# Attention and FP4 feed-forward on one core: side products spread over the slots of the attention loop

## The chip, the cores and the metric

The kernel runs on one core of one Trainium2 chip. The metric is the time of one execution on the device in microseconds (us), the median of several. Within the core, five engines run their own instruction streams in order and meet at semaphores: TensorE (PE in the profile; its weight loads are PEld), VectorE (DVE), ScalarE (ACT), GpSimd (POOL) and SyncE (SP), whose queue issues nearly all DMA transfers here.

## The reference, cut to what matters

The input is x of 4 batches x 2048 rows x 256 columns, in float32. Multi-head attention (16 heads of 16) with rotary tables on all rows but the first 679, a residual, a layer norm, then a gated feed-forward whose operands are first rounded to FP4 values in blocks of 16, a residual and a second layer norm:

```python
qkv = (x @ w_qkv + b_qkv)                  # 256 -> 3 * 256, then q and k are rotated
attn = softmax(q @ k.T / sqrt(16))         # per batch and head: 2048 x 2048
x = layernorm(x + (attn @ v) @ w_proj + b_proj)
def fp4_linear(x, w): return fp4_quant_dequant(x) @ fp4_quant_dequant(w).T
gate, y = fp4_linear(x, w_gate), fp4_linear(x, w_up)          # 256 -> 704
x = layernorm(x + fp4_linear(silu(gate) * y, w_down))         # 704 -> 256
```

The rounding divides each block of 16 by a sixth of its largest magnitude, snaps to the grid 0, 0.5, 1, 1.5, 2, 3, 4, 6 and multiplies back.

## The kernel before, in words

**The main loop.** Attention is cut into 64 *items* (the list `items`, built just after `first_rest`), 16 for each batch: an item is two heads by two chunks of 512 queries, or in the last batch four heads by one chunk. An item walks through 16 key tiles, `kt` = 0 to 15. For one `kt` the loop issues on TensorE two pairs of score matmuls (`mm2`, L243 to L249), then the weighing of the *previous* key tile by v (`weigh`, L1113, four float32 matmuls that the trace shows as eight records) into the bank `po`, then four matmuls of the row maxima of the *next* items (`maxima`, L883). ScalarE takes the exponentials of the scores (L1363) and a copy for the maxima (L922), VectorE the maxima (L925, L930). Scores and maxima use six PSUM banks in turn (`bank()`, pool `ps_r`). One more bank, `side` (pool `ps_f`, one buffer), belongs to the side work. The eighth is `po`.

**The side work.** Everything else is written as Python generators, the *streams*, and woven into the loop while the program is being built: the projections of q, k and v for the next batch (`prepare`, `project_units`, `project_qk`, `cut_out`, `project_v`), the FP4 weights (`prepare_weights`), the shifts and sums of the attention (`shift`, `keep`), and the output projection and feed-forward of tiles of 128 rows (`feed_forwards` L1084, `attended` L978, `feed_forward` L1005; five such streams, NFF). The order on every engine is what the Python order says (a manual schedule). `Side.call` (L118) is called once per key tile, between the first and the second score pair; it steps each stream whose due time has come, and a stream runs until its next `yield`, which tells when it wants to be called again. The clock for that, `pace.now`, is a planner's running estimate and not the chip's. So a call may put several products of several streams on TensorE, or none.

**Banks of the side products.** A stream that wants to multiply asks `side_bank` (L205). It gets the side bank if the planner thinks it free. If it isn't, the stream yields and asks again; after PATIENCE (3000 on the planner's clock) it takes a bank of the ring of six instead. `side_done` marks when the side bank will have been read.

**One feed-forward tile** takes on TensorE, in this order: the output projection (six matmuls of 256 columns), a transpose pair, three gate and up products (twelve matmuls each, two of 256 columns and one of 192, L1029), six transposes in two goes, and the down projection (seventeen matmuls in two halves with a `yield` between, in one bank, L1052 to L1060). Between them GpSimd and VectorE quantize (L424 to L477): on GpSimd the product with the inverse (L458), an add, a subtract and a product with the scale.

**Deadlines.** `need(i)` (L1263) starts the loads of item i while item i - 2 runs, as soon as all the head groups of item i have been projected, or at kt = NEED_BY = 7 (L1335). If the projections aren't done then, `side.drain` (L130) steps the streams alone, with no score matmuls between, until they are. Items of the last batch (48 to 63) take key columns of all four head groups. At the end of the loop a last drain finishes the feed-forward; there, warming matmuls on `po` fill the pauses.

Of the kernel before, what the change touches and what calls it, by code (L numbers as in the profile page):

```python
# [55 lines left out]
class Pace:  # L56
# [4 lines left out]
    def __init__(self):  # L61
        self.now = 0.0
        self.spent = {"pe": 0.0, "v": 0.0}
        self.free = {"v": 0.0, "s": 0.0, "g": 0.0, "d": 0.0}
# [31 lines left out]
class Side:  # L96
# [3 lines left out]
    def __init__(self, pace):  # L100
        self.pace = pace
        self.streams = []
        self.room = {}
        self.rest = lambda ns: None

    def add(self, gen, first=False, margin=lambda: MARGIN):
# [11 lines left out]
    def call(self, room=ROOM):  # L118


        now, spent = self.pace.now, self.pace.spent
        self.room = {k: min(self.room.get(k, 0.0) + room, ROOM_MOST) for k in spent}
        for e in list(self.streams):
            if e[1] <= now and (e[2] or min(self.room.values()) > 0.0):
                before = dict(spent)
                self.step(e)
                for k in spent:
                    self.room[k] -= spent[k] - before[k]

    def drain(self, until=lambda: False):  # L130
        while self.streams and not until():
            e = min(self.streams, key=lambda e: e[1])
            self.rest(e[1] - self.pace.now)
            self.pace.now = max(self.pace.now, e[1]) + 100.0
            self.step(e)
# [3 lines left out]
def tile_attn_fp4ffn_postln(  # L139
# [44 lines left out]
    NU = H  # L184
# [5 lines left out]
    pace = Pace()  # L190
    side = Side(pace)
# [7 lines left out]
    def bank():  # L199

        return ps_r.tile([P, QW], F32, tag="bank", name="bank")

    at_item, side_free = [0], [0.0, None]

    def side_bank():  # L205


        patience = pace.now + PATIENCE
        while at_item[0] < len(items) and pace.now < side_free[0]:
            if pace.now > patience:  # L210
                return bank()
            yield (min(side_free[0], pace.now + 1000.0),)
        if at_item[0] == len(items):
            return bank()
        side_free[:] = 1.0e12, ps_f.tile([P, QW], F32, tag="side", name="side")
        return side_free[1]
# [11 lines left out]
    def mm(out, lhsT, rhs, start, stop):  # L228
        nc.tensor.matmul(out, lhsT=lhsT, rhs=rhs, start=start, stop=stop)  # L229
        n = int(np.prod(rhs.shape[1:]))  # L230
        pace.pe(n / 0.6 + 10.0 if rhs.dtype == F32 else n / 2.4 + 12.0)

    def mm3(out, lhsT, rhs):


        n = len(lhsT)
        for k in range(n):
            (ah, al), (bh, bl) = lhsT[k], rhs[k]
            mm(out, ah, bh, k == 0, False)
            mm(out, ah, bl, False, False)  # L240
            mm(out, al, bh, False, k == n - 1)
# [14 lines left out]
    def flip(out, in_, idn):  # L256
        nc.tensor.transpose(out, in_, idn)  # L257
        pace.pe(165.0)
# [55 lines left out]
    def wide_tile(tag, dtype=F32, cols=FC * P):  # L314
        return ff_tile(tag, cols, dtype)
# [421 lines left out]
    def first_rest():  # L737
# [25 lines left out]
    items = [(b, h0, f) for b in range(1) for h0 in range(0, H, 2) for f in range(2)]  # L763
    items += [(b, h0, f) for b in range(1, B - 1) for f in range(2) for h0 in range(0, H, 2)]
    items = [
        (b, tuple((h0 + s, 2 * f + r) for r in range(2) for s in range(2))) for b, h0, f in items
    ]
# [188 lines left out]
    def cuts(u, tag):  # L956
        t = wide_tile(f"{tag}{u}", F32R)
        return [t[:, k * C : (k + 1) * C].rearrange("p (c n) -> p c n", c=CC) for k in range(2)]
# [46 lines left out]
    def feed_forward(u, b, t, xr, fast=False, claim=lambda: None):  # L1005


        yield (yield from normalize(u, xr, fast))
        dq = wide_tile(f"qy{u}")[:, :C]
        yield from quantize(u, xr, dq, P, C // BLK, fast)  # L1010
        pt = yield from side_bank()
        for c in range(CC):
            flip(pt[:, c * P : (c + 1) * P], dq[:, c * P : (c + 1) * P], ident)
        xqT = cuts(u, "qy")
        halve(xqT, pt[:, :C].rearrange("p (c n) -> p c n", c=CC))
        r = side_done(pt, pace.v(C, pace.s(C)))
        xqT = [[a[:, c, :] for a in xqT] for c in range(CC)]
        yield r

        h = wide_tile(f"h{u}")[:, :FF]  # L1020
        th = wide_tile(f"qm{u}")[:, :FF]

        for c0 in range(0, FF, HQ):
            n = min(HQ, FF - c0)
            cols = slice(c0, c0 + n)
            pt = yield from side_bank()
            pg, pu = pt[:, :n], pt[:, HQ : HQ + n]
            for m, p in enumerate((pg, pu)):
                mm3(p, xqT, [[w[:, m, c, cols] for w in wgu] for c in range(CC)])  # L1029
            nc.scalar.activation(th[:, cols], pg, AF.Tanh, scale=0.5)  # L1030
            r = pace.s(n)
            nc.vector.scalar_tensor_tensor(th[:, cols], th[:, cols], 1.0, pg, ALU.add, ALU.mult)
            pace.v(n, r)
            nc.vector.scalar_tensor_tensor(h[:, cols], pu, 0.5, th[:, cols], ALU.mult, ALU.mult)  # L1034
            side_done(pt, pace.v(n))
            yield
        hq = wide_tile(f"qy{u}")
        yield from quantize(u, h, hq, P, FF // BLK, fast, KL // BLK)
        hqT = [
            wide_tile(f"{k}{u}", F32R).rearrange("p (f t) -> p f t", f=FC) for k in ("h", "qm")  # L1040
        ]
        for f0 in range(0, FC, TQ):
            pt = yield from side_bank()
            n = min(TQ, FC - f0)
            for f in range(n):
                flip(pt[:, f * P : (f + 1) * P], hq[:, (f0 + f) * P : (f0 + f + 1) * P], ident)
            halve(
                [a[:, f0 : f0 + n, :] for a in hqT],
                pt[:, : n * P].rearrange("p (f t) -> p f t", f=n),
            )  # L1050
            r = side_done(pt, pace.v(n * P, pace.s(n * P)))
            yield  # L1052
        yield r
        pt = yield from side_bank()
        for f in range(FC - 1):
            if f == FC // 2:
                yield
            for a, w in ((0, 0), (0, 1), (1, 0)):
                mm(pt[:, :C], hqT[a][:, f, :], wd[w][:, f, :], (f, a, w) == (0, 0, 0), False)
        mm(pt[:, :C], hqT[0][:, FC - 1, :], wd[0][:, FC - 1, :], False, False)  # L1060
        mm(pt[:, :C], hqT[1][:KL, FC - 1, :], wd[0][:KL, FC - 1, :], False, True)
        nc.vector.tensor_tensor(xr, pt[:, :C], xr, ALU.add)
        side_done(pt, pace.v(C))
        r = (yield from normalize(u, xr, fast)) + 1000.0
        yield
        after = claim()
        yield r
        move(out[b, t * P : (t + 1) * P, :], xr)
        return after
# [373 lines left out]
```

## Time and profile before

| | before |
|---|---|
| three runs | 3644.8, 3641.26, 3633.11 us; median 3641.26 |
| the profiled execution | 3633.82 us, its span 3632.0 us |
| TensorE busy | 3420.8 us, 94% of the span |
| ScalarE busy | 2901.6 us, 80% |
| VectorE busy | 2731.4 us, 75% |
| GpSimd busy | 1503.3 us, 41% |
| mean granted clock of TensorE | 0.977 |

The span is from the first to the last instruction of one execution. Busy times of engines overlap. In a row of the profile, L246 is line 246 of the kernel; `bank<-qp,kp` names the tile written and those read: `bank<-qp,kp` are scores, `bank<-kp,qp` maxima, `po<-pr,vp` the weighing, `side<-` or `bank<-` with `wgu` gate and up, with `wd` down, with `wp` the output projection, with `wqk` and `wv` the projections. An `x4` merges neighbours alike. The granted clock is 1 or 0.5 at a time, and means in between are averages over a window.

### The profile page before, as it was taken

Reading aid. Unit: us, or ns where it says so; the run is one execution under the profiler, and the core shown is the slowest. Engines: PE = TensorE matmul, PEld = TensorE weight load, DVE = VectorE, ACT = ScalarE, POOL = GpSimd, SP = SyncE. Lnnn points to the kernel's source line nnn. Section 1 sums busy time; section 2 is a strip of 40 time slices with the busy share of each in tenths; the row PEclk is TensorE's granted clock in tenths of the full one; section 3 lists DMA queues with packets and bytes.
Section 4 is the critical chain, followed back from the end, with each engine's and each line's share of the span. In section 5 each row is a group of like instructions: output and inputs, shape, how many; then the busy total and the mean of one; then the engine's idle time right before and its main releaser. Section 6 shows DMA issues by size and latency. Waiting matters only on the chain.

```text
span 3632.0 us, 63611 instructions
## 1 busy us (share of the span) xinstructions
PE 3420.8 (94%) x21870; PEld 1648.0 (45%) x21870; DVE 2731.4 (75%) x6433; ACT 2901.6 (80%) x5800; POOL 1503.3 (41%) x1762
## 2 busy tenths in 40 slices
PE   7999899988999999999999999999998999999998
PEld 3333343433445444444444544444443444544457
DVE  4767677767677878887878788777777887888757
ACT  2889799979988878787888888888788887877871
POOL 4234423241245555553445455455321334453354
PEclk7999999999999999999999999999999999999999
DMA  5223323324323424232232323424334443424300
GB/s 140 62 74 79 87 71 72 81 70 75 76 65 79 91 52 87 59 84 42 55 75 68 75 65 74 86 65 86 60 61 80 85 75 60 84 57 77 68 13 19
DMA packets 216231, 257.42 MB, mean 71 GB/s; under 512 B 80728, under 2 KB 162200, under 8 KB 209176
## 3 DMA queue, kind: packets, MB, share of 16 engines
q1 hardware_dynamic: 215908, 253.36, 32.8%
q8 instruction: 173, 2.83, 0.4%
q14 instruction: 150, 1.23, 0.1%
HBM read 163.99 MB, written 76.28 MB: 66 GB/s over the span
## 4 chain that ended last, share of the span: by engine, by line
PE 78%; DVE 12%; ACT 5%; DMA 2%; issue 2%; POOL 1%; SPq 1%; ACTq 0%; DVEq 0%; POOLq 0%
PE bank L246 33%; PE po L1113 26%; PE side L229 13%; DVE mx L930 6%; ACT more L922 4%; PE bank L229 4%; PE side L257 2%; DVE more L925 1%; PE bank L257 1%; ACT pr L1363 1%; SPq L253 1%; DVE qm L464 1%; DVE qm L466 1%; DVE sc L447 0%; DMA kp<-qk 0%
## 5 line engine op out<-in xcount | busy, mean ns | idle before, releaser
L1363 ACT ACTIVATE pr<-bank 128x512 f32<-128x512 f32 x4096 | 2192.7, 611 | 123.4 <-PE bank L246 109.4
L930 DVE TENSOR_REDUCE mx<-bank 128x1 f32<-128x512 f32 x2048 | 1355.1, 686 | 632.8 <-PE bank L246 627.7
L246 PE MATMUL bank<-qp,kp 50*128 50x512 f32 (+1 forms) x3616 | 924.6, 451 | 97.1 <-DVE mx L930 53.9
L1113 PE MATMUL po<-pr,vp 128*17 128x512 f32 x6912 | 975.4, 607 | 0.3 <-ACT pr L1363 0.3
L922 ACT ACTIVATE more<-bank 128x512 f32<-128x512 f32 x1024 | 616.7, 603 | 271.0 <-PE bank L246 251.2
L925 DVE CUSTOM_DVE_ANT_0 more<-bank,more 128x512 f32<-128x512 f32 x1024 | 691.9, 681 | 30.1 <-ACT more L922 24.1
L246 PE MATMUL bank<-kp,qp 48*128 48x512 f32 x3584 | 689.4, 454 | 19.5 <-DMA qp<-first 8.5
L246 PEld LDWEIGHTS bank<-kp,qp 48*128 48x128 f32 x3584 | 283.5, 188 | 795.1 <-ACT pr L1363 393.1
L246 PEld LDWEIGHTS bank<-qp,kp 50*128 50x128 f32 x3616 | 451.5, 186 | 420.4 <-DVE mx L930 133.8
L458 POOL TENSOR_TENSOR qy<-qy,qm 128x704 f32<-128x704 f32 (+4 forms) x292 | 334.6, 1146 | 557.8 <-DVE qm L466 514.6
L1113 PE MATMUL po<-pr,vl 128*17 128x512 f32 (+1 forms) x1408 | 223.1, 562 | 3.8 <-ACT pr L1363 3.8
L229 PE MATMUL side<-wgu,qy 128*128 128x256 f32 (+1 forms) x1584 | 220.4, 288 | 5.5 <-DVE xr L1002 4.2
L1113 PEld LDWEIGHTS po<-pr,vp 128*17 128x17 f32 x6912 | 120.1, 95 | 214.7 <-issue 213.8
L229 PEld LDWEIGHTS side<-wgu,qy 128*128 128x128 f32 x1584 | 194.9, 191 | 47.2 <-issue 26.2
L946 POOL TENSOR_SCALAR rs<-mv 128x1 f32<-128x1 f32 x128 | 29.6, 232 | 361.3 <-DVE mv L944 323.2
L246 PE MATMUL bank<-qp,kl 50*128 50x512 f32 (+1 forms) x544 | 144.5, 451 | 18.1 <-DVE mx L930 9.8
L458 POOL TENSOR_TENSOR qy<-h,inv 128x704 f32<-128x704 f32 (+1 forms) x66 | 90.1, 1365 | 170.9 <-PE bank L246 78.2
L950 POOL TENSOR_SCALAR xr<-xr,mv,rs 128x256 f32<-128x256 f32 x120 | 149.7, 1247 | 13.1
L458 POOL TENSOR_TENSOR qy<-qy,sc 128x704 f32<-128x704 f32 (+4 forms) x146 | 137.7, 943 | 11.4
L458 POOL TENSOR_TENSOR qy<-xr,inv 128x256 f32<-128x256 f32 (+1 forms) x64 | 39.2, 612 | 227.7 <-DVE inv L449 193.5
L994 POOL TENSOR_TENSOR xr<-xr,bp 128x256 f32<-128x256 f32 x64 | 47.0, 735 | 206.1 <-DMA xr<-in_x_dram 187.7
L229 PE MATMUL side<-wd,h 128*128 128x256 f32 x550 | 114.8, 299 | 0.3 <-DVE h L1034 0.3
(177 smaller groups left out, 3381.3 us busy)
## 6 DMA issues: line engine op xcount, KB each, us to landing
kp<-qk SPq DMA_DIRECT2D x288, 160.0 KB
kl<-qk SPq DMA_DIRECT2D x96, 160.0 KB
vp<-v SPq DMA_DIRECT2D x104, 136.0 KB
qk<-part SPq DMA_DIRECT2D x102, 128.0 KB
o<-raw SPq DMA_DIRECT2D x96, 128.0 KB
qk<-q SPq DMA_DIRECT2D x96, 128.0 KB
qp<-qk SPq DMA_DIRECT2D x192, 64.0 KB
rot<-q SPq DMA_DIRECT2D x90, 128.0 KB
```

What stands on the lines that cost most here:

```text
L229: nc.tensor.matmul(out, lhsT=lhsT, rhs=rhs, start=start, stop=stop)
L246: mul = nc.tensor.matmul(out, lhsT=lhsT, rhs=rhs, start=True, stop=True)
L253: hold(nc.sync.dma_start(out=out, in_=in_))
L257: nc.tensor.transpose(out, in_, idn)
L458: engine.tensor_tensor(out[:, k0:k1], in0[:, k0:k1], in1[:, k0:k1], op)
L922: nc.scalar.activation(more[s], pm, AF.Relu)
L925: nc.vector.tensor_tensor_reduce(more[s], pm, more[s], 1.0, -3.0e38, ALU.add, ALU.max, mx[:, s, t, kc : kc + 1])
L930: nc.vector.tensor_reduce(mx[:, s, t, kc : kc + 1], pm, AX.X, ALU.max)
L950: nc.gpsimd.tensor_scalar(y, y, mv[:, 0:1], rs, ALU.subtract, ALU.mult)
L994: hold(nc.gpsimd.tensor_tensor(xr, xr, bp, ALU.add))
L1113: mul = nc.tensor.matmul(po[32 * j : 32 * j + DV, (half or 0) * HQ :][:, :n], lhsT=vals[i][j][:, kt, :], rhs=prs[j], start=(kt == 0), stop ...
L1363: nc.scalar.activation(pr, scs[s], AF.Exp, scale=SCALE)
```

## The change

A counter `visits` is added to `Side`. Each call sets it to 0, and a stream that gets a bank, or takes a ring bank after its patience, adds 1. While the loop runs, `side_bank` lets a stream go on only if nobody has had a bank in this call (`visits` is 0) and the side bank is free; the fallback to a ring bank has the same condition, and a waiting stream asks again after 500 on the planner's clock instead of at the time at which the bank comes free, 1000 at most. So a call puts products of one stream at most on TensorE, apart from the second half of a down projection, which asks for no bank. And in `feed_forward` a `yield` stands between the gate's six matmuls and the up projection's six, which count as a visit of their own; both write halves of the same bank. In the last 16 items (the last batch) that `yield` is left out. A drain steps streams with `visits` at 0 each time.

```diff
@@ class Side
+        self.visits = 0
@@ def call
+        self.visits = 0
@@ def drain
             e = min(self.streams, key=lambda e: e[1])
+            self.visits = 0
@@ def side_bank
-        while at_item[0] < len(items) and pace.now < side_free[0]:
-            if pace.now > patience:
+        while at_item[0] < len(items) and (pace.now < side_free[0] or side.visits > 0):
+            if pace.now > patience and side.visits == 0:
+                side.visits += 1
                 return bank()
-            yield (min(side_free[0], pace.now + 1000.0),)
+            yield (pace.now + 500.0,)
+        side.visits += 1
         if at_item[0] == len(items):
             return bank()
@@ def feed_forward
             for m, p in enumerate((pg, pu)):
+                if m and at_item[0] < len(items) - NU:
+                    yield
+                    side.visits += 1
                 mm3(p, xqT, [[w[:, m, c, cols] for w in wgu] for c in range(CC)])
```

## The prediction

> **What bounds the kernel now.** I read the page first (busy time, the chain that ended last), then the TensorE timeline slot by slot. Below, a *slot* is one key tile of one attention item: eight TensorE records of the weighing (L1113) to the next eight.
>
> ```profile
> PE 3420.8 (94%) x21870; PEld 1648.0 (45%) x21870; DVE 2731.4 (75%) x6433; ACT 2901.6 (80%) x5800; POOL 1503.3 (41%) x1762
> ...
> PE 78%; DVE 12%; ACT 5%; DMA 2%; issue 2%; POOL 1%; SPq 1%; ACTq 0%; DVEq 0%; POOLq 0%
> PE bank L246 33%; PE po L1113 26%; PE side L229 13%; DVE mx L930 6%; ACT more L922 4%; PE bank L229 4%; PE side L257 2%; DVE more L925 1%; PE bank L257 1%; ACT pr L1363 1%; SPq L253 1%; DVE qm L464 1%; DVE qm L466 1%; DVE sc L447 0%; DMA kp<-qk 0%
> ```
>
> The chain is TensorE for 78%, so a slot's length is nearly what TensorE does in it. But not always. Two slots from the TensorE timeline (start, length, engine, line, tiles; in brackets the idle time before and what ended it), the first without a side product, the second with one of twelve matmuls (gate and up):
>
> ```profile
> 390.98 1.05 PE L1113 MATMUL po<-pr,vp 128*17 128x512 f32 x8
> 391.96 0.73 PE L246 MATMUL bank<-kp,qp 48*128 48x512 f32 x4
> 392.53 0.41 PE L246 MATMUL bank<-qp,kp 50*128 50x512 f32 x2
> 393.14 0.63 PE L246 MATMUL bank<-qp,kp 50*128 50x512 f32 x2 [0.20 <-ACT more L922]
> 393.71 1.05 PE L1113 MATMUL po<-pr,vp 128*17 128x512 f32 x8
> ```
> ```profile
> 1714.98 1.05 PE L1113 MATMUL po<-pr,vp 128*17 128x512 f32 x8
> 1715.96 0.73 PE L246 MATMUL bank<-kp,qp 48*128 48x512 f32 x4
> 1716.62 1.67 PE L229 MATMUL side<-wgu,qy 128*128 128x256 f32 x12
> 1718.22 0.73 PE L246 MATMUL bank<-qp,kp 50*128 50x512 f32 x4
> 1718.89 1.05 PE L1113 MATMUL po<-pr,vp 128*17 128x512 f32 x8
> ```
>
> The empty slot takes 2.73 us: ScalarE needs that much (four exponentials at 0.535 from L1363's 2192.7 us over 4096, one copy at 0.603). TensorE alone would need about 2.24 (0.98 weighing, 1.26 for the eight score and maximum matmuls). So an empty slot wastes 0.5 us of TensorE; a full one takes 3.91 us and wastes nothing.
>
> **The change, part by part.** I counted side products per slot in the built program's order of instructions, before and after, and gave each class the mean length that such slots have in the trace of before (full granted clock only). Side work is priced by spacing in the timeline: 0.134 us a matmul of 256 columns (1.60 for twelve), 0.118 of 192, 0.24 of 512, 0.145 a transpose. Slots of items 17 to the middle of 63 (743; after, 742 and one that stands alone below):
>
> - none: 238 before, 134 after, 2.85 us
> - one or two transposes: 81, 102, 2.87
> - about 0.58 us: 56, 50, 2.99
> - six matmuls, 0.80 us: 54, 233, 3.36
> - 0.85 to 1.3 us: 91, 68, 3.58
> - 1.3 to 1.5: 65, 65, 3.98
> - twelve matmuls, 1.6 us: 102, 62, 3.98
> - 1.65 to 2.0: 17, 17, 4.32
> - 2.0 to 2.4: 12, 9, 4.63
> - above, two products in one slot: 27, 2, 5.03
>
> **Term 1, evening out.** Change in count times length, in the order of the list: -296 + 60 - 18 + 602 - 82 + 0 - 159 + 0 - 14 - 126 = -33 us. With medians instead of means it is -44. I take -38. Bounds: if a half product cost only TensorE's own 2.24 + 0.80 = 3.04 us in place of 3.36, 233 x 0.32 = 75 us more is gained (-108); if its extra readers make such slots 3.51 (the upper quartile of the 67 such slots in the trace), 233 x 0.15 = 35 eats the gain (0).
>
> **Term 2, the queue before batch 3.** The polling rule moves other streams too. The last two of the 16 query-key projections of batch 3 stand in slots 711 and 712 before, and in 737 and 741 after. At item 46, kt 7 (NEED_BY, L1335) need(48) wants every group of batch 3. Before, they are long done. After, the planner drains the side streams there: 156 side matmuls stand on TensorE between two halves of slot 742 with no score or weighing between, 20.5 us at the prices above, ending in the wp product of tile 4 of batch 2. The trace has such a drain twice, at items 6 and 14. The first, as a row of the windows view and its TensorE timeline:
>
> ```profile
> 393.70:419.90 26.20, 13.07 (x53) 7.92 (x55) 8.98 (x21) 4.92 (x10) 20.04 (x22) 0.67 0.24 70
> ```
> ```profile
> 397.85 1.67 PE L229 MATMUL side<-x,wqk 128*128 128x512 f32 x6 [0.83 <-ACT q L555]
> 401.94 0.56 PE L257 MATMUL side<-ident,qy 88*128 88x88 f32 x2 [2.43 <-POOL qy L458]
> 403.36 1.07 PE L229 MATMUL side<-wv,x 128*128 128x256 f32 x3 [0.86 <-DVE wgu L413]
> 411.95 0.80 PE L229 MATMUL side<-wv,x 128*128 128x256 f32 x2 [7.53 <-POOL x L410]
> ```
>
> The reader should see the 7.53 us behind POOL and 20.04 of 26.20 us of POOL. POOL sets a drain: 26.2 against its 20.0, in the second drain 17.3 against 15.4. So I add what POOL must do, in its order, before that last wp product: two h*inv at 1.389; normalize of two tiles at 0.232 + 0.575 + 1.247; two rotations at 1.287 + 1.301 + 1.286; one 256-wide quantizing tail at 2 x 0.736 + 0.622; two 704-wide ones at 0.29 + 2 x 1.696 + 1.392; one cut at 0.611 + 1.281; two attended stages at 0.735 + 0.400 + 0.735 + 0.735. Sum 34.0. With the 2 to 6 us that the two known drains are longer than POOL, the slot takes 38 us. Bounds: 21 (TensorE's matmuls alone) and 50 (34 plus all 16 us of waits between reader and next product on the one side bank: some 20 products at the 0.68 to 0.95 us seen in the drains). Its 20.5 us of products are missing from the other slots; term 1 has that already.
>
> **Term 3, ring banks that are held.** A product that finds the side bank taken takes one of the six ring banks after PATIENCE. If it is finished in a later slot, scores and maxima run on five. The trace shows what that does (a down projection that holds a ring bank from 3247.5):
>
> ```profile
> 3248.75 0.50 PE L246 MATMUL bank<-qp,kl 50*128 50x512 f32 x2
> 3249.18 1.05 PE L1113 MATMUL po<-pr,vl 128*17 128x512 f32 x8
> 3250.16 0.73 PE L246 MATMUL bank<-kp,qp 48*128 48x512 f32 x4
> 3250.73 0.40 PE L246 MATMUL bank<-qp,kl 50*128 50x512 f32 x1
> 3252.35 1.10 PE L246 MATMUL bank<-qp,kl 50*128 50x512 f32 x3 [1.23 <-DVE mx L930]
> ```
>
> The first score pair comes apart: its second half waits for a bank that a maximum still reads. Before, 9 products hold a ring bank over a slot's end; the 20 slots after their first exceed max(2.76, 2.33 + side work) by 0.54 to 1.44 us, mean 0.83 and nine tenths under 1.05, where other slots of the stage exceed it by 0.12; those that end in the next slot (3) exceed it by 0.62. After, 49 products do (30 of them split gate and up products, 19 down projections), with 66 such slots: 35 more of the short kind at 0.50 and 11 more of the long at 0.70 is 25; 40 more first slots at about 0.1 is 4. I take +28. Bounds: 46 x 0.42 = 19 and 46 x 0.93 + 6 = 49.
>
> **Term 4, behind the drain.** The last unit's cut stands on POOL behind that wp product (1.389 + 2.05 + 1.89 = 5.3 us), SP's queue holds its stores before the 24 loads of item 48, and the maxima of item 48 start four slots, 12 us, later. DMA steps in the chain last 3 to 6 us each. I take +4, bounds 0 and 12. The main loop's restart: the slot after the second drain took 8.0 us against some 3.6, after the first none was lost; +2, bounds 0 and 5.
>
> **Nothing** for the rest: the same side products run in all, the last drain has 131 warming matmuls in place of 134, and no instruction is new.
>
> One rule against the row. In the 743 slots 75 us run at half the granted clock, which costs at most 37 us. From 447.2 to 788.2 us 82 of 118 slots are empty, TensorE idles briefly in each, and the granted clock is 1.00; so I give fewer empty slots no gain of clock. The Trainium skill (TensorE: Matmul & The Clock Gate, A second HAM failure mode) says that frequent short idling between groups, banks cycling, makes the clock oscillate. By it the change could win back up to those 37 us and the sum would be -3; by the row it is what follows.
>
> **Sum:** -38 + 38 + 28 + 4 + 2 = +34 us on the profiled execution's own 3633.82 us (span 3632.0): 3668. That execution lies 7.4 us under the median of the three runs, 3641.26, inside their spread (3633.11 to 3644.8). A difference goes on the median: 3675 us.
>
> **The rivals.**
>
> *Faster: half products run at TensorE's own pace.* Term 1 becomes -108, the sum -108 + 72 = -36, 3605 us. It decides below 3.15 us a half-product slot (233 x 0.21 = 49 us under the mean's -33, against 72). For it: the second half has its operands in place. Against it: of the 67 slots with six matmuls in the trace nine tenths took over 3.21.
>
> *No change.* The terms cancel: a drain near 21 us with a held bank at its lower price, -38 + 21 + 19 + 6 = +8, 3649 us. For it: the drain's POOL work partly runs in any case. Against: both known drains end with POOL.
>
> *Much slower: the drain is a stop for loads too.* Drain 50, held banks 49, loads 12, restart 5, evening out at -33: +83, 3724 us. For it: TensorE at half clock in drains (0.67 above). Against: all upper ends together.
>
> *The change does nothing:* the order denies it: 27 slots with two products become 2.
>
> **How the numbers follow.** Chances: forecast (3653 to 3700) 0.60; much slower 0.15; no change 0.12; faster 0.13. Within 0.3% (11 us), about what a measurement can tell from no change: 0.12. Slower 0.75, faster 0.13. The range leaves out the outer half of the faster case and the top of the much slower one: 3625 to 3718; the forecast's own is 3653 to 3700.
>
> **What would show it.** In the changed profile: a stretch near item 46 of some 38 us with no L1113, POOL nearly full; six-matmul slots at 3.2 to 3.4 us; far more single score matmuls followed by a wait on mx or more; items 17 to 45 faster by some 20 us in all, net of held banks. Wrong if the drain hardly stops TensorE, if half-product slots fall under 3.15, or if a held side bank stalls what I priced at nothing.

## The result and the profile after

| | before | after |
|---|---|---|
| median, shortest and longest | 3639.91 (3633.11 to 3644.8) | 3738.43 (3730.24 to 3741.96) |
| span of the profiled execution | 3632.0 us | 3728.5 us |
| mean granted clock of TensorE | 0.977 | 0.965 |

The ratio is 1.0256, 95% interval 1.0233 to 1.028: the change costs 98.5 us. I had said 3675, with a range of 3625 to 3718. The sign was right, the size was not: +34 us were forecast, +98.5 came. (The kernel before has four runs here, one more than ahead of the prediction.)

The page of the changed kernel has the same engines' busy times and nearly the same chain by engine:

```profile
PE 3482.6 (93%) x21867; PEld 1667.6 (45%) x21867; DVE 2739.5 (73%) x6432; ACT 2908.3 (78%) x5800; POOL 1510.0 (40%) x1763
...
PE 77%; DVE 11%; ACT 5%; issue 2%; DMA 2%; POOL 1%; SPq 1%; POOLq 0%; ACTq 0%; DVEq 0%
```

TensorE is busy 62 us longer with the same matmuls (three records fewer), so part of the loss is its own clock. The shares tell no more. A ledger by slots does: the slots' lengths in the changed trace less those of before, slot by slot, add up to the 96.4 us between the two spans. Slot n starts with the n-th weighing, so items 17 to 45 are slots 273 to 736; where the expectations below say "between slots 272 and 1014", they count from 0 and mean 273 to 1015.

| stretch | after less before, us |
|---|---|
| start and slots 1 to 272 | +2.9 |
| slots 273 to 736 (items 17 to 45) | -19.5 |
| slots 737 to 741 | +0.1 |
| slot 742 (the drain) | +50.9 |
| slots 743 to 768 (behind it, items 46 and 47) | +22.5 |
| slots 769 to 800 (items 48 and 49) | +32.6 |
| slots 801 to the end | +6.9 |

The gain is there. A slot with half a gate and up product, from the changed kernel's TensorE timeline (start, length, engine, line, tiles):

```profile
1724.46 1.05 PE L1121 MATMUL po<-pr,vp 128*17 128x512 f32 x8
1725.44 0.73 PE L251 MATMUL bank<-kp,qp 48*128 48x512 f32 x4
1726.02 0.40 PE L251 MATMUL bank<-qp,kp 50*128 50x512 f32 x2
1726.35 0.97 PE L234 MATMUL side<-wgu,qy 128*128 128x256 f32 x6
1727.25 0.50 PE L251 MATMUL bank<-qp,kp 50*128 50x512 f32 x2
1727.68 1.05 PE L1121 MATMUL po<-pr,vp 128*17 128x512 f32 x8
1728.66 0.73 PE L251 MATMUL bank<-kp,qp 48*128 48x512 f32 x4
```

From weighing to weighing such a slot takes 3.2 us; the mean over those of items 17 to 63 is 3.34, the median 3.22 (3.36 forecast). But there is the drain. Its row of the windows view (length, then busy time of TensorE, weight loads, VectorE, ScalarE and GpSimd, then the granted clock) and that of 31.55 us within it, its TensorE timeline with the idle time and its releaser in brackets, and some rows of GpSimd and VectorE:

```profile
2576.00:2629.70 53.70, 33.41 (x178) 26.62 (x178) 26.28 (x59) 6.72 (x16) 43.79 (x48) 0.66 0.15 45
2595.43:2626.98 31.55, 20.49 (x91) 16.73 (x91) 10.19 (x23) 3.39 (x8) 29.74 (x33) 0.61 0.11 36
```
```profile
2587.62 0.58 PE L234 MATMUL side<-wd,qm 64*128 64x256 f32 x1
2595.43 0.69 PE L262 MATMUL side<-ident,qy 128*128 128x128 f32 x2 [7.24 <-POOL qy L463]
2597.09 2.93 PE L234 MATMUL side<-wgu,qy 128*128 128x256 f32 x12 [0.96 <-DVE qy L418]
2601.40 1.65 PE L234 MATMUL side<-wgu,qy 128*128 128x256 f32 x12 [1.39 <-DVE h L1042]
...
2626.98 1.62 PE L234 MATMUL side<-wp,h 128*128 128x256 f32 x6 [0.61 <-POOL q L418]
...
2637.82 1.12 PE L262 MATMUL side<-ident,qy 128*128 128x128 f32 x4 [5.59 <-POOL qy L463]
...
2656.74 0.76 PE L251 MATMUL bank<-kl,qp 48*128 48x512 f32 x1 [5.18 <-DMA qp<-qk]
```
```profile
2594.76 0.62 POOL L463 TENSOR_TENSOR qy<-qy,sc 128x256 f32<-128x256 f32 x1
...
2617.62 0.73 POOL L418 TENSOR_TENSOR h<-qy,h 128x256 fp32r<-128x256 f32 x1
...
2625.60 1.27 POOL L418 TENSOR_TENSOR q<-q,part 128x512 fp32r<-128x512 f32 x1
```
```profile
2626.41 0.42 DVE L1070 TENSOR_TENSOR xr<-side,xr 128x256 f32<-128x256 f32 x1 [3.77 <-PE side L234]
```

The clock is 0.66 over the stretch: the same twelve matmuls take 2.93 us at half clock and 1.65 at full. GpSimd is busy 43.8 of 53.7 us, as the forecast wanted, but it ends only one wait of TensorE, the 7.24 us up to 2595.43. The waits behind that, 11 us in nine pieces, end with VectorE, when it has read the side bank. That holds for the last one too, though the view puts it down to GpSimd's `q` (the cut, which ended at 2626.87): the `wp` product reads `h`, which GpSimd had written by 2618.35, and VectorE had read the side bank by 2626.83. Behind the drain two more waits stand, 5.59 us for GpSimd, which still has quantizing to do, and 5.18 us for the loads of item 48's maxima.

The held banks look like those in the trace of before. A down projection took a ring bank in the slot before (at 1695.66 us); the first score pair comes apart, and its second half waits for a maximum:

```profile
1697.36 1.05 PE L1121 MATMUL po<-pr,vp 128*17 128x512 f32 x8
1698.34 0.73 PE L251 MATMUL bank<-kp,qp 48*128 48x512 f32 x4
1698.91 0.40 PE L251 MATMUL bank<-qp,kp 50*128 50x512 f32 x1
1699.62 0.50 PE L251 MATMUL bank<-qp,kp 50*128 50x512 f32 x1 [0.31 <-DVE mx L935]
1700.05 0.98 PE L234 MATMUL side<-wgu,qy 128*128 128x256 f32 x6
```

And there is something that the forecast gave nothing for. With *excess* as what a slot takes above its floor, max(2.76, 2.33 + its side work), the slots 273 to 1015 without the drain divide so (number and sum of the excess, us). A held bank's *first* slot is the one in which a product takes a ring bank, its *following* ones those up to the product's second half:

| slots | before | after |
|---|---|---|
| touched by half clock | 24: 39.8 | 38: 81.0 |
| first slot of a held bank, full clock | 9: 1.4 | 48: 18.7 |
| following slots of it, full clock | 20: 16.6 | 65: 50.3 |
| all others | 690: 79.6 | 591: 87.3 |

So outside the drain 51 us more go to held banks and 41 us more to slots at half clock. Against these, the floors sum to 64.9 us less. With the drain's 53.6 and 7.7 more in all other slots, that is 88.7 us; another 7.7 lie ahead of slot 273 and behind 1015.

### The profile page after: what moved, and what is told of

It reads as the page before. It is cut to its first block, busy times and chain, and to the rows that moved or that the text cites. A ratio compares the mean times of both kernels' runs of the same rounds, so it can differ in the third digit from the quotient of the medians.

```text
span 3728.5 us, 63674 instructions
## 1 busy us (share of the span) xinstructions
PE 3482.6 (93%) x21867; PEld 1667.6 (45%) x21867; DVE 2739.5 (73%) x6432; ACT 2908.3 (78%) x5800; POOL 1510.0 (40%) x1763
## 4 chain that ended last, share of the span: by engine, by line
PE 77%; DVE 11%; ACT 5%; issue 2%; DMA 2%; POOL 1%; SPq 1%; POOLq 0%; ACTq 0%; DVEq 0%
PE bank L251 32%; PE po L1121 25%; PE side L234 13%; DVE mx L935 6%; PE bank L234 4%; ACT more L927 4%; PE side L262 2%; DVE more L930 1%; PE bank L262 1%; SPq L258 1%; DVE qm L471 1%; ACT pr L1371 1%; DVE qm L469 1%; DVE sc L452 0%; DMA v<-vst 0%
## 5 line engine op out<-in xcount | busy, mean ns | idle before, releaser
L463 POOL TENSOR_TENSOR qy<-qy,qm 128x256 f32<-128x256 f32 (+4 forms) x292 | 335.7, 1150 | 556.1 <-DVE qm L471 507.1
L234 PE MATMUL side<-wgu,qy 128*128 128x256 f32 (+1 forms) x1644 | 250.5, 295 | 3.7 <-DVE h L1042 2.8
L234 PEld LDWEIGHTS side<-wgu,qy 128*128 128x128 f32 x1644 | 210.0, 193 | 70.5 <-issue 53.5
L262 PE MATMUL side<-ident,qy 128*128 128x128 f32 (+1 forms) x454 | 90.2, 299 | 25.9 <-POOL qy L463 15.3
L567 POOL TENSOR_TENSOR rot<-rot,tab 128x512 f32<-128x512 f32 x45 | 58.0, 1289 | 138.4 <-DMA rot<-q 136.9
```

Source lines behind the costliest of these rows:

```text
L463: engine.tensor_tensor(out[:, k0:k1], in0[:, k0:k1], in1[:, k0:k1], op)
L567: hold(tt.tensor_tensor(rot, rot, sin_sb, ALU.mult))
```

## The experiments

The theory after the result: drain, held banks and the clock, in this order of size. Times are medians; each ratio is to the kernel before on the same chip in the same minutes, where its median was 3639.8 to 3645.1 us, so that a difference between two rows is good to some 5 us. "No drain" below means that no drain stands at item 46.

| run | edit | us | ratio, 95% |
|---|---|---|---|
| e1 | changed, projections exempt from the asking rule | 3684.9 | 1.0092 to 1.0151 |
| e2 | changed, split only in the side bank | 3669.72 | 1.0064 to 1.0098 |
| e3 | one stream per call alone | 3635.79 | 0.9971 to 1.0003 |
| e4 | split alone | 3667.68 | 1.0051 to 1.0085 |
| e5 | before, with a drain | 3680.53 | 1.0069 to 1.0143 |
| e6 | before, with held banks | 3662.44 | 1.0032 to 1.0071 |
| e7 | changed, no drain, no held bank | 3594.52 | 0.9837 to 0.9892 |
| e8 | changed, no held bank, projections due earlier | 3599.9 | 0.9847 to 0.9905 |
| e9 | changed, scales interleaved | 3731.22 | 1.0217 to 1.0288 |
| e10 | before, no held bank | 3644.11 | 0.998 to 1.0013 |
| e11 | e7, scales interleaved | 3592.89 | 0.9834 to 0.9887 |
| e12 | changed, shorter quantizer | 3639.3 | 0.9981 to 1.0012 |
| e13 | before, shorter quantizer | 3577.77 | 0.9802 to 0.9858 |
| e14 | e1, shorter quantizer | 3605.29 | 0.9877 to 0.9911 |
| e15 | e7, shorter quantizer | 3550.78 | 0.9717 to 0.977 |
| e16 | e6, shorter quantizer | 3613.02 | 0.9893 to 0.9939 |

### One part at a time

e1 lets the projections ask by the old rule, so that they are done before item 46:

```diff
@@ def side_bank
-        while at_item[0] < len(items) and (pace.now < side_free[0] or side.visits > 0):
-            if pace.now > patience and side.visits == 0:
+        while at_item[0] < len(items) and (pace.now < side_free[0] or side.visits > 0 and not soon):
+            if pace.now > patience and (soon or side.visits == 0):
@@ def project_qk, def project_v
-        pt = yield from side_bank()
+        pt = yield from side_bank(True)
```

> The changed kernel, but the query-key and value projections are exempt from the rule of one stream per call (they still wait for the side bank). The built order then has the last projections of batch 3 in slots 701 and 704 (737 and 741 in the change) and no drain at item 46; it keeps 232 slots with a half product (233) and 44 products that hold a ring bank (49). Theory D (the late projections: the drain at item 46 with what follows it is most of the loss): slot classes at the mean lengths of before give -12 us, held banks +35, so about +23 us on before, 3660 to 3670 us. Theory P (the half products themselves cost, and the drain only moves side work from other slots): still at least +70 us, 3710 us or more.

Slot 742 falls from 53.6 us to an ordinary one, and the whole run is 53.5 us shorter than the changed kernel. That is more than the forecast's own price on the same footing: the 20.5 us of side products return to other slots (the classes of slots lose 21 us of their 33), so 38 + 6 - 21 = 23 was forecast. Yet 45 us are still lost, and 3684.9 lies between what theory D allowed and the 3710 of theory P.

e2 splits a gate and up product only if it has the side bank; down projections still hold a ring bank.

```diff
-                if m and at_item[0] < len(items) - NU:
+                if m and pt is side_free[1] and at_item[0] < len(items) - NU:
```

> The changed kernel, but gate and up are put in two calls only when they have the side bank; a product in a ring bank stays whole. The order keeps the drain at item 46 (18.7 us of products, 20.5 in the change) and 236 half-product slots; 18 products hold a ring bank instead of 49. If a held ring bank costs what it did in the traces (0.65 us for a following slot, 0.25 for a first one), 45 following slots and 31 first ones fewer give -37 us on the change: about 3700 us. If held banks cost nothing: 3738 us as the change.

69 us less than the changed kernel where the counts gave 37, although the drain stays (54.4 us in slot 742). Half clock in all slots falls from 206 to 163 us (36 and 42 us of it in the drain). Held banks cost more than their own slots show. And slots 743 to 768 lose 4.3 us here, not 22.5, so what stood behind the drain belongs to the changed kernel's order and not to a drain as such.

e3 takes the asking rule alone, without the split:

```diff
-                if m and at_item[0] < len(items) - NU:
-                    yield
-                    side.visits += 1
```

> Half of the change: one stream per call, gate and up together in one slot as before. The order has no drain at item 46 (last projections in 705 and 710), 13 held ring banks (9 before) and 84 half-size slots. Theory D and theory P both expect it near before: slot classes -9 us, held banks 0: 3625 to 3640 us. If waiting for a call of one's own is itself what costs (late streams everywhere), 3680 us or more.

e4 is the kernel before with the split alone:

```diff
+                if m and at_item[0] < len(items) - NU:
+                    yield
```

> The other half: gate and up in two calls, but the old rule for asking (several streams may have a bank in one call). The order has no drain at item 46, but 60 products hold a ring bank for 90 following slots (before 9 and 20). Slot classes +8 us, held banks +58: about +66 us, 3700 us, though nothing is late. If held banks cost nothing: about 3648 us. Theory P expects a loss too, but per half product, of which this kernel has fewer (176 slots): some +50 us.

e3 is as fast as before, as expected: no drain, 13 held first slots. e4 has no drain either, so the drain takes both parts: one stream per call, and a second visit for each gate and up product. e4 loses 28 us, which none of the forecasts had (3700 with the slots' price, 3648 with none, some +50 by theory P): its 81 following slots have 64.6 us of excess, 48 more than before, but the slots without a held bank have 25 less.

### The two suspects alone, and both away

e5 is the kernel before with `PITCH_QK = 44000.0` in place of 34000.0. e6 gives every down projection's first half a ring bank:

```diff
         yield r
-        pt = yield from side_bank()
+        pt = bank()
```

> The kernel before with one number changed (PITCH_QK 34000 to 44000), so that the late projections come due closer to their need. Neither the asking rule nor the split of the change is in it; the order of the program then has 14.5 us of side products in the slot ahead of weigh 743, where the last of item 46's projections are drained (the changed kernel has about 18 us there, the kernel before 0), 13 held first slots and 30 following ones (9 and 20 before), and the classes of slots are worth -8 us by the table. Theory D (a drain costs its helpers' chain on POOL and ScalarE and a stretch behind it at a poor overlap, far more than its products; the changed kernel's took 53.6 us for 18 us of products, and +23 us more lay in the 25 slots behind it): a slot of 36 to 46 us, +10 to +25 behind it, so 3675 to 3705. Rival P (a drain costs its products, the rest was the split or the asking): 14.5 us less the 2.5 us an ordinary slot holds, so 3645 to 3655.

> The kernel before with one line changed: every down projection's first half goes to a bank of the score ring and is held over a yield, where before only those that found the side bank taken did. No asking rule, no split, no drain. First slots of a held bank 57 (9 before), following ones 75 (20). Theory H (a held ring bank costs 0.775 us in each following slot and 0.39 in a first one, as the changed kernel's slots show): 55 x 0.775 + 48 x 0.39 = 61 us, and the classes of slots give +8, so about 3700, 3690 to 3710. Rival R (the held banks stand where slots are long anyway, so that other waits go away in exchange, as in the split-alone run, where 61 more following slots raised the sum of these by 48 us and the other slots lost 25): 3665 to 3685. Rival N (a held bank costs nothing, the long slots have another cause): 3640 to 3650.

The drain's price is confirmed in kind: 35 us with one number changed, from 14.5 us of products (20.5 in the changed kernel, not 18). The 10 to 25 us expected behind it did not come: slots 743 to 768 take 0.7 us more. Its windows row and its TensorE timeline:

```profile
2589.42:2631.60 42.18, 25.66 (x130) 20.42 (x134) 23.13 (x50) 5.52 (x13) 27.22 (x29) 0.72 0.07 23
```
```profile
2601.23 2.93 PE L229 MATMUL side<-wgu,qy 128*128 128x256 f32 x12 [1.18 <-DVE qy L413]
2608.67 2.93 PE L229 MATMUL side<-wgu,qy 128*128 128x256 f32 x12 [4.52 <-DVE h L1034]
2612.99 2.87 PE L229 MATMUL side<-wgu,qy 128*128 128x192 f32 x12 [1.39 <-DVE h L1034]
```

GpSimd is busy only 27 of 42 us here: this drain is not GpSimd's. TensorE, at half clock, and VectorE, which reads its bank, take turns, as in the second part of the changed kernel's. A list of GpSimd's work does not give a drain's length.

The held banks alone came out at 17 us, between what rival R and rival N gave: the 74 following slots have the excess expected (54.5 us against 16.6), but the other slots lose 18 and those at half clock 8.

e7 takes the drain and every held bank out of the changed kernel (e1's edit, e2's edit and the line below for the down projection); e8 does without e1's edit, with `PITCH_QK = 30000.0`:

```diff
-            if f == FC // 2:
+            if f == FC // 2 and pt is side_free[1]:
```

> The changed kernel with both suspects taken out: the projections' helpers ask by the old rule (no drain at item 46), and a call yields between its halves only if it has the side bank, for the split and for the down projections too (no ring bank is held over a yield: 0 first and 0 following slots, 9 and 20 before). The one-stream rule and the split where the side bank is free stay. The classes of slots are worth -21 us against the kernel before by the table, the held banks that are gone -15, so -37. If drain and held banks are all that the change lost: 3595 to 3615, below both kernels. If the half-clock stretches that the runs with more evenly placed side work showed (163 to 206 us of slots at half clock against 164 before; 18.7 to 50 us lost to it) return with it: 3615 to 3640. If the two suspects are not the cause: 3660 or more.

> The changed kernel with no ring bank held over a yield (as in the run beside it), the asking rule in force for the projections too, and PITCH_QK 34000 lowered to 30000, so that the late projections come due earlier and their drain at item 46 is gone. 113 empty slots, 252 with half products and 86 with whole ones between slots 272 and 1014; classes of slots -24 us against the kernel before, held banks -15, so -39; the deferred work behind item 47 ends the kernel some 10 us later (side work in the last slots 85 us against 72), half of which may show. If drain and held banks are all that the change lost: 3595 to 3620. If half-clock stretches return: 3620 to 3645. If neither: 3660 or more.

Both are faster than both kernels, e7 by 50 us against before and by 144 against the change. The TensorE timeline of e7 at slot 742:

```profile
2550.85 1.05 PE L1121 MATMUL po<-pr,vp 128*17 128x512 f32 x8
2551.83 0.73 PE L251 MATMUL bank<-kp,qp 48*128 48x512 f32 x4
2552.40 1.22 PE L251 MATMUL bank<-qp,kp 50*128 50x512 f32 x4
2553.55 1.05 PE L1121 MATMUL po<-pr,vp 128*17 128x512 f32 x8
```

An empty slot of 2.7 us stands where the drain was. So what the change lost goes with the drain and the held banks, and not with the half products, which e7 keeps (theory P). But the sum does not go by slots: with e1 in between, the drain is worth 53.5 us and the held banks 90.4 us, where their slots' excess in e1 is 60.4. (The table of classes gives 9 of the 90 to other places of the products.) e10 shows the other side; it is the kernel before with the edit of the down projection alone:

> The kernel before with one line changed: a down projection yields between its halves only if it has the side bank, so no ring bank is held over a slot (0 first and 0 following slots, 9 and 20 before; between slots 272 and 1014 the classes of slots stay within 2 us). Theory H (0.83 us a following slot, 0.15 a first one, as the kernel before's slots show): -16 to -18 us less 2 for longer slots, 3622 to 3630. Rival R (other slots lengthen in exchange, as the held-alone run's others shortened by 18 us when it added 54 following slots: a net price near 0.4 us a following slot): -5 to -9, 3631 to 3640. Rival N (held banks cost nothing): 3640 to 3647.

Nothing, as rival N said (the interval leaves 7 us at most), although the 18.0 us of excess in held slots go; in the profile, slots at half clock take 21 us more (39.8 to 60.8). That need not be the edit's doing. The kernel before took 3630.68 us at a mean granted clock of 0.979 in one run and 3661.3 at 0.968 in another, so half clock differs that much from run to run, and the profile of before is one of its faster runs. The held banks are thus worth 0, 17 or 90 us in three places, with 20, 54 and 55 following slots at stake.

### Where the half clock comes from

In the changed kernel and in e1 half-clock stretches stand where no bank is held. One of them, at 2115.6 us: TensorE, VectorE and GpSimd.

```profile
2112.71 0.50 PE L251 MATMUL bank<-kp,qp 48*128 48x512 f32 x1
2114.55 1.10 PE L251 MATMUL bank<-kp,qp 48*128 48x512 f32 x3 [1.34 <-DVE mx L935]
...
2117.46 1.91 PE L1121 MATMUL po<-pr,vp 128*17 128x512 f32 x8
```
```profile
2110.72 1.43 DVE L452 TENSOR_SCALAR sc<-sc 128x16 f32<-128x16 f32 x1
2112.19 0.25 DVE L453 RECIPROCAL inv<-sc 128x16 f32<-128x16 f32 x1
2112.47 1.43 DVE L454 TENSOR_SCALAR inv<-inv 128x16 f32<-128x16 f32 x1
2113.82 1.27 DVE L935 TENSOR_REDUCE mx<-bank 128x1 f32<-128x512 f32 x2
```
```profile
2110.44 3.43 POOL L463 TENSOR_TENSOR qy<-qy,qm 128x704 f32<-128x704 f32 x2 [5.62 <-DVE qm L471]
```

The reader should see three steps: VectorE's multiplication of 16 columns takes 1.43 us, where most take 0.18, while GpSimd works on another stream's tile; the maxima come behind it; TensorE waits 1.34 us for them, and then the weighing takes 1.91 us in place of 1.05. I counted TensorE's pauses of over 1 us that begin outside half clock and drains in slots 273 to 1015: 9 before, 15 after, 16 in e1, 4 in e7, and 139 in the 18 profiles. Behind 98 of these a half-clock stretch begins within 7 us; behind 41 none does. Of the 15 in the changed kernel, 13 end with VectorE; the other two are the waits behind the drain.

e9 tried the first step, with the scales and their inverses in turn in one buffer:

```diff
-        sc = ff_tile(f"sc{u}", FF // BLK)[:, :nb]
-        inv = ff_tile(f"inv{u}", FF // BLK)[:, :nb]
+        both_ = ff_tile(f"sc{u}", 2 * (FF // BLK))
+        sc, inv = both_[:, : 2 * nb : 2], both_[:, 1 : 2 * nb : 2]
```

> The changed kernel with the quantizer's block scales and their inverses interleaved in one buffer, so that VectorE's two short multiplications on them (128x16 and 128x44) step by two; order, products and waits stay. In the changed kernel 26 of the 236 such instructions between slots 272 and 1014 take over 0.9 us where most take 0.17 (16 of 236 in the kernel before), each of the 26 while a GpSimd instruction runs; 29 us of VectorE time, and 10 of the 17 half-clock stretches there begin within 9 us of one. Theory S (a short VectorE multiplication that waits for a GpSimd instruction makes the score maxima late, TensorE pauses 1 to 2 us, and the clock halves): the long ones go, half clock in the slots falls from 206 us to some 130, and the time by 20 to 45 us, to 3693 to 3718. Rival T (they only stand beside the pauses): 3728 to 3742. Rival U (a step of two does not change what they wait for): 26 long ones stay, 3733 to 3742.

> The run without held banks and without a drain (3594.52 us) with the interleaved scales of the run beside it as well. That run has 8 long multiplications, 8 us of VectorE time, and 20 us of half clock between slots 272 and 1014. Theory S: little is left to gain, 3585 to 3593. Rivals T and U: 3591 to 3599. More than 3605 if the interleaved operands are slower on VectorE or GpSimd.

Rival U holds: 24 long multiplications are left of 26, and the times stay within the spread of the runs without it (3731.22 against 3738.43, 3592.89 against 3594.52). The experiment failed to take the long multiplications away, so it says nothing on theory S. The Trainium skill could have told me (VectorE: DVE Perf Modes, What auto-detection actually checks): the mode that uses both ports asks for one source and a destination in SBUF and for the sizes of the outer dimensions, and it names no step among its conditions; the 24 long ones agree.

e12, e13 and e14 shorten VectorE's quantizing instead, and leave part of the computation out for that:

```diff
-        nc.vector.tensor_scalar(inv[:rows], inv[:rows], 1.0 - 2.0**-22, None, ALU.mult)
...
-        nc.vector.tensor_scalar(m.bitcast(I32), y[:, :n].bitcast(I32), EXPO, None, ALU.bitwise_and)
-        nc.vector.tensor_scalar(m, m, 1.0, 1.5 * 2.0**22, ALU.max, ALU.mult)
+        nc.vector.tensor_scalar(m, y[:, :n], 1.0, 1.5 * 2.0**22, ALU.max, ALU.mult)
```

> The changed kernel with a shorter quantizer on VectorE: the multiplication of the inverse scales by 1 - 2^-22 and the mask of the exponent bits are left out (the rounding step is then taken from the value itself, so part of the computation is missing); 130 x 2 instructions of VectorE fewer, some 100 us of its 2740 us. The order of the products on TensorE stays. Outside half clock and the drain the changed kernel has 15 TensorE pauses of over 1 us between slots 272 and 1014, 12 of them with a half-clock stretch within 7 us behind (9 and 6 in the kernel before), with about 2.3 us of quantizing on VectorE in the 4 us ahead. Theory V (VectorE, kept by the quantizers of two streams, gives the score maxima late, TensorE pauses, the clock halves): 4 to 9 pauses, half clock in the slots 206 us to 110 to 150, and 25 to 50 us off: 3688 to 3713, where the kernel before loses 5 to 20. Rival W (the pauses are not VectorE's): 3720 to 3742, pauses and half clock as before.

> The kernel before with the same shorter quantizer (the same part of the computation left out). 9 pauses, 6 of them ahead of a half-clock stretch, 75 us of half clock between slots 272 and 1014 (111 in all slots). Theory V: 3 to 6 pauses, 5 to 20 us off: 3620 to 3638. Rival W: 3633 to 3645. Should it gain as much as the changed kernel, VectorE's lateness has no part in what the change cost.

> The changed kernel with the old asking rule for the projections (3684.9 us, no drain, 43 held products and 55 following slots, 16 pauses with 13 half-clock stretches behind, 185 us of half clock in the slots) and the shorter quantizer. Theory V: 4 to 9 pauses, half clock 90 to 130 us, 30 to 60 us off: 3625 to 3655, and what is left above the run with neither holds nor drain (3594.52 us) is the direct price of the held banks. Rival W: 3670 to 3690.

All three gain more than any theory said: 99, 63 and 80 us. The changed kernel's page then has VectorE at

```profile
PE 3427.8 (94%) x21867; PEld 1652.8 (45%) x21867; DVE 2618.9 (72%) x6140; ACT 2899.8 (79%) x5800; POOL 1502.3 (41%) x1763
```

which is 121 us less VectorE work, and 55 us less of TensorE with the same matmuls. Pauses fall from 15 to 7 (those that end with VectorE from 13 to 5), half clock in the slots from 206 to 115 us, excess of slots at half clock from 81.0 to 37.8; the excess of following slots stays (50.3 and 51.1). So theory V is right in kind: less quantizing on VectorE takes away most of the pauses, and half clock goes with them. Rival W falls. That the pauses make the half clock rests on their order in time; no run makes a pause alone. Nor is the clock all of the gain: 25 us of the changed kernel's come in slots at full clock without a held bank, and in the kernel before 28 there against 21 at half clock. Theory V is wrong in size, since the kernel before gains too: the changed kernel's own share of it is 99 - 63 = 36 us of its 98.5.

e15 and e16 repeat e7 and e6 with the shorter quantizer:

> The run without held banks and without a drain (3594.52 us) with the shorter quantizer on VectorE (the same part of the computation left out). The kernel before with it takes 3577.77 us, the run with held banks but no drain 3605.29. With fewer pauses to start half-clock stretches, slot classes and held banks should add up: -21 for classes and -15 for the 9 first and 20 following slots that are gone, -37 against 3577.77: 3535 to 3550, which makes the held banks of the run with them worth 55 to 70 us (52 more by the prices of 0.39 and 0.77). Rival R (other slots lengthen where no bank is held): 3555 to 3575.

> The held-alone run (3662.44 us, 17 us above the kernel before, where prices and classes gave 56) with the shorter quantizer. Against 3577.77 us of the kernel before with it. If held banks alone cost little because the slots that hold are VectorE-bound anyway, then with a relieved VectorE they cost nearer their full price: 3610 to 3635. If other waits shrink in exchange whatever VectorE does (rival R): 3590 to 3605. If a held bank costs nothing by itself: 3575 to 3588.

| against the kernel before with the same quantizer, us | full | shorter |
|---|---|---|
| held banks alone (e6, e16) | +17 | +35 |
| changed, no drain, no held bank (e7, e15) | -50 | -27 |
| held banks put back (e1 less e7, e14 less e15) | +90 | +55 |
| drain put back (changed less e1, e12 less e14) | +53 | +34 |
| all of the change | +98.5 | +61.5 |

e16 lies where relieved VectorE time was to put it; e15 ends 1 us above its range, and the held banks at 54.5 us just below theirs. With the clock mostly quiet (no slot of e15 between 273 and 1015 is at half clock) the held banks of the changed kernel cost 55 us; e14's held slots show 61. That they are so near is partly chance: e14's slots at half clock have 16 us, and its other slots 19 us less than e15's, as rival R said. With the full quantizer 36 us come on top in the changed kernel, where slots at half clock have 89.2 us of excess in e1 and 12.5 in e7; in e6 18 go away. What decides how many pauses an order of the program makes, I could not settle: a held bank lies at the pause itself in one of the 15, and the number goes from 3 (e6) to 16 (e1) with much the same held banks. It belongs to the order: e9, with the changed kernel's order of the products, has the same 15 and 12, e11 the 4 of e7.

## Why the prediction was right or wrong

By the slots of the two profiles, the sum of +34 us went wrong here:

| term of the sum | forecast | measured |
|---|---|---|
| evening out and held banks (-38 + 28): slots at full clock | -10 | -6 |
| the drain's slot | 38 | 53.6 |
| behind the drain (4 + 2), and nothing for the clock: excess of slots at half clock, the waits in them included | 6 | 41.2 |
| ahead of slot 273 and behind 1015 | 0 | 7.7 |

So the step that failed is above all "nothing" for the clock, with the little that was given for the restart behind the drain; after it comes the price of the drain, whose mechanism was wrong for more than half of its length.

**Evening out (-38) and held banks (28): right together.** Half-product slots took 3.34 us against 3.36 priced. The count of held banks was 49 products and 66 following slots, and the trace has 48 and 65 at full clock. A following slot's excess is 0.775 us (0.83 before), a first one's 0.39, which I put at 0.1, so held slots have 51 us more excess where I said 28; but the floors and the other slots gave 57 us where I said 38. That items 17 to 45 gained 19.5 us, where "some 20" was said, is in part luck: their slots at full clock gained 36.9, and half clock took 17.4 back. With the quiet clock the removal of the held banks is worth 55 us, with the real one 90. Freed of its costs, the change gives -50 (e7), against -37 expected for that order.

**The drain (38, bounds 21 to 50): right in place, wrong in mechanism.** It took 53.6 us. "POOL sets a drain" holds for the first 19.4 us: GpSimd began its list only at 2582.4 us, 6.4 us into the slot, and TensorE waited for it until 2595.43. From there to the last `wp` product, 31.55 us, TensorE and VectorE took turns on the one side bank: 20.5 us of TensorE for products that the forecast's spacing prices at 12.0, since 24.7 us of the stretch ran at half clock, and 11 us of waits. The scores add 2.7. My upper bound had the waits on the side bank but no half clock. GpSimd's list of 34.0 us did take 36.6, and 7.8 us of other streams' work followed before the last `wp` product; that their sum comes near the slot's length is a coincidence, because that product waited for VectorE. This is read from the trace; no run shortens GpSimd's work in the drain. e5's drain, 42.2 us with 27.2 of GpSimd, says the same: the rule "26.2 against 20.0, so GpSimd sets a drain" was read from too few drains.

**Behind the drain (4 + 2).** Slots 743 to 768 took 22.5 us more. I had priced the main loop's restart by an earlier drain (0 to 5); here TensorE waited 5.59 us for GpSimd's remaining list and 5.18 us for the loads of item 48, and 25 us of these slots' time ran at half clock. With e2's order the same stretch lost 4.3 us, with e5's 0.7.

**Nothing for the clock: wrong.** I set the row (empty slots at full clock) against the Trainium skill's rule of frequent short idling (TensorE: Matmul & The Clock Gate, A second HAM failure mode) and gave neither gain nor loss. The changed kernel has 100 empty slots less and lost clock: 206 us of slots at half clock in place of 111. Neither reading has it. The empty slots' idling of 0.2 to 0.3 us does no harm (the granted clock is 1.00 from 447.2 to 788.2 us); it is behind single pauses of over 1 us that half clock begins, and these the forecast did not look for. It asked how much idle time goes, and should have asked which pauses come.

Of the rivals, "much slower" at 3724 named the drain at its upper end and loads behind it and came nearest; it still lacked the clock. The 32.6 us in items 48 and 49 I had only in part: the floors there rise by 12.4 for side products that the asking rule put off, which the table of classes has; slots at half clock take another 12.5 (with the shorter quantizer and the same order the stretch costs 19.1).

## What to carry to other kernels

When work is spread more evenly over a pipeline's slots, list what must be finished by a deadline and where its last item now stands; a stretch in which the main loop stops for it took 2.6 to 2.9 times its products here (53.6 us for 20.5, 42.2 for 14.5), and in one order out of three it left late loads and half clock behind it. Do not price such a stretch by the engine that is busiest in it: ask what ends each wait. Do not pay for the spreading with a buffer of the ring that the main loop lives on: here splitting only what has the spare bank and letting the projections ask first turned +98.5 us into -50. And a price read from slots is good only while no pause of over a microsecond comes with it, so ask of each new alignment of two side streams what it does to the engine that feeds the main loop.

## What the runs showed of the hardware that I had not expected

- **Half clock follows a short pause, and lasts.** 98 of 139 pauses of TensorE of 1 us and more were followed within 7 us by stretches of 3.4 to 24 us at half clock, nearly all of 14 us or less. The Trainium skill's page on TensorE: Matmul & The Clock Gate (HAM oscillation) speaks of idle gaps of more than about 3.4 us; here half clock followed one of 1.34 us, and TensorE was 58% busy in the 3.4 us before it began.
- **VectorE waits for GpSimd whole instructions.** Of 236 multiplications of 16 or 44 columns, 26 in the changed kernel took 1.32 us on average where the 191 short ones took 0.18. Each of the 26 overlaps a GpSimd instruction and ends 29 to 44 ns after one. The Trainium skill's page SBUF — State Buffer (SBUF: two separate sides) says that the two share a port pair as an exclusive lock for a whole instruction, and the rows agree with it.
- **An engine at 75% busy was worth its work.** Some 113 us less on VectorE (2731.4 to 2618.5) gave 63 us in the kernel before, whose chain has VectorE at 12% (6% at most in one line). The chain shows who came last, not who made it late.
